# A scan's state ring widened from 8 to 16 tiles with borrowed rows, its read-outs set four slots later

## The chip, the cores and the metric

The kernel runs on one core of a Trainium2 chip. The core has five engines, each with its own instruction stream that is worked in order: TensorE (PE, matmuls; its weight loads are listed apart as PEld), VectorE (DVE), ScalarE (ACT), GpSimd (POOL) and SyncE (SP), which here only issues DMA transfers. They meet through semaphores. The metric is the time of one execution on the device in microseconds (us); a profiled execution gives the time of every instruction beside it.

## The reference

Input x is 32 sequences of 256 tokens of 256 features. A gated state-space block (a scan over time) is computed first, then two layers of windowed attention with a feed-forward part; the result is added to x. Only the scan matters here:

```python
def step(h, inputs):
    ad, bd, xt, ct = inputs
    h = jnp.clip(h * ad[:, :, None] + bd[:, :, None] * xt[:, None, :], -10.0, 10.0)
    yt = jnp.einsum('bd,bdh->bh', ct, h)
    return (h, yt)
_, ys = jax.lax.scan(step, h0, (Ad..., Bd..., xn..., Cm...))
y = ys.transpose(1, 0, 2) + D * xn
return y * jax.nn.silu(gate) @ W_out.T
```

The state h is 16 x 512 for each sequence. The 256 steps of a sequence depend on one another; the read-out yt of a step needs only that step's state.

## The kernel before

**Groups.** The 32 sequences are worked in four groups of eight (`GB = 8`). The 16 states of 8 sequences fill the 128 partitions, so one step of one group is one VectorE instruction on a 128x512 tile (`step`, line 719; line 722 in the profile). The first group's scan runs by itself ("alone": `g == 0`), before any attention can start; the scans of the other groups run beside the attention and feed-forward of the group before. The kernel has a second branch (`exact`) that these inputs don't take.

**Slots.** A scan is laid out in slots, one per step. `group_scan` fills an agenda: `at(s, what, ...)` puts a piece of work into slot s, and `scan_slots` calls the pieces slot by slot. A scheduler then places each instruction in its engine's order; it may move an instruction from where it was called, except where `tc.keep_in_program_order` holds it. 32 steps make a chunk (`CH = 32`, eight chunks c = 0 to 7, s0 = 32 c); 16 steps make a half chunk (hb).

**A step.** SP loads a row of the normalised input from DRAM, spread over 128 partitions (`load_rows`, line 691, tile xrep, six buffers); two of every eight rows are spread by TensorE instead (`spread_rows`, line 699, tile bx, from a transfer xq, line 751). ScalarE scales it (`scale_row`, line 712). VectorE adds the state and clips (line 722): a new state tile h from pool `hp`, eight buffers. The step t of a new state can start only when the tile it takes has been read out. The clip limits (`lim`, lines 666 and 667) are made on POOL once per chunk.

**Read-out.** Four steps make a block i. `read_out` (line 729, matmul in line 734) issues four matmuls, one for each state of the block, each 32 columns of weights wide, so that each lands in its own 32 rows of the bank y. In the profile an fp32 matmul is two records, so a block is eight. The call stood in slot s + 4 i + 5, where s is the first slot of the half chunk: one slot after the block's last step. The weights `ly` are written by POOL (`put_c`, line 675), one tile for each half.

**What follows a read-out.** POOL multiplies the input by D (`skip`, line 764, reads xq, writes xd, which has one buffer), VectorE adds y (`gated`, line 785), TensorE turns the tile (`out_turn`, line 791, tile tz), VectorE multiplies by the gate sg (`out_gate`, line 805, tile zT), TensorE projects (`project_y`, line 814), ScalarE copies (`copy_y`, line 825) and issues the transfer to ys in DRAM (`put_y`, line 836). The gate sg is written by ScalarE (`gate_th`, through `reorder`, line 373) into one buffer per chunk.

**Beside it on TensorE in the first scan.** The input projections of the chunk (`project`, line 401) and those of the other three groups, done ahead (`ahead_project`, line 428, tile ps_a, loaded on SP by line 417); the raw projections (line 520), the turns for the normalisation (line 550) and sums (line 624) of the next chunk. The convolution of the next chunk is on POOL (line 480) and VectorE (lines 474 and 491), its statistics on VectorE (line 560) and POOL (line 567), its normalisation on ScalarE and POOL (lines 581, 588, 589). The tiles xq and xa share four buffers of tag "rot".

**Residual rows.** Attention keeps one tile `res0` to `res7` per sequence of the group (`load_res`, line 960), 2 x 257 columns of 128 partitions, in pool `rpool`, loaded from ys after slot 256 + 18 (`DRAIN`). During the first scan they hold nothing.

Of the kernel before, what the change touches and what calls it, by code (L numbers as in the profile page):

```python
# [10 lines left out]
FP = mybir.dt.float32  # L11
# [8 lines left out]
P = 128  # L20
S = 256
DM = 256
KM = DM // P
DI = 512
# [4 lines left out]
NCH = S // CH  # L29
# [44 lines left out]
def kernel(  # L74
# [29 lines left out]
    nc = tc.nc  # L104
# [119 lines left out]
    def program(ctx, exact):  # L224
        rpool = ctx.enter_context(tc.tile_pool(name="res", bufs=1, reuse_waits="tile"))
# [3 lines left out]
        hp = ctx.enter_context(tc.tile_pool(name="hp", bufs=8, reuse_waits="tile"))  # L229
# [6 lines left out]
        def bank(pool, tag, name):  # L236
            return pool.tile([P, DI], FP, tag=tag, name=name)
# [141 lines left out]
        def group_scan(g):  # L379
# [8 lines left out]
            alone = g == 0  # L388

            agendas = [{}]  # L390
            state = {"p": one}
            ck = [{} for _ in range(NCH)]

            def at(s, what, *args):
                agendas[-1].setdefault(s, []).append(partial(what, *args))

# [288 lines left out]
            def by_tensor(t):  # L685
                return alone and t % (2 * NQ) < XR
# [31 lines left out]

            def step(c, t):
                bx = ck[c].pop(("rep", t))  # L720
                h_new = hp.tile([P, DI], FP, tag="h", name="h")
                nc.vector._custom_dve(  # L722
                    TENSOR_ADD_SAT, out=h_new, in0=state["h"], in1=bx,
                    s0=ck[c]["lim"][:, 0, t : t + 1], s1=ck[c]["lim"][:, 1, t : t + 1],
                )
                ck[c]["h", t] = state["h"] = h_new


            def read_out(c, hb, i):
                if i == 0:  # L730
                    ck[c]["y", hb] = bank(ps_w, "w", "y")
                for q in range(NQ):
                    t = i * NQ + q
                    nc.tensor.matmul(  # L734
                        ck[c]["y", hb][32 * q : 32 * q + 32, :],
                        ly[hb % 2][:, 32 * t : 32 * t + 32],
                        ck[c].pop(("h", hb * TB + t)),
                        start=(i == 0),
                        stop=(i == NI - 1),
                    )  # L740

            def load_skip(c, hb):
                if alone:
                    xd = ap_.tile([P, HEADS, DH], FP, tag="rot", name="xq", bufs=4)
                    ck[c]["xq", hb] = xd
                    xd = xd.rearrange("p h d -> p (h d)")
                else:
                    xd = ck[c]["xd"] = sp.tile([P, DI], FP, tag="xd", name="xd")
                for q in range(NQ):
                    t0 = hb * TB + q  # L750
                    nc.sync.dma_start(
                        out=xd[q * 32 : (q + 1) * 32],
                        in_=rows(c)[:, t0 : t0 + TB - NQ + 1 : NQ, :].rearrange(
                            "b i d -> i b d"
                        ),
                    )
# [96 lines left out]

            rep_w = []
            at(-1, start)
            if alone:
                at(-30, spread_weights)
                constants(at)
            for c in range(NCH):
                for t in range(CH):  # L860
                    at(c * CH + t, step, c, t)
            for c in range(NCH):
                s0 = c * CH
                for hb in range(CH // TB):
                    s = s0 + hb * TB
                    for i in range(NI):
                        at(s + 4 * i + 5, read_out, c, hb, i)
                    at(s + 21, gated, c, hb)
                    at(s + 25, out_gate, c, hb)
                    at(s + 11, skip, c, hb)  # L870
                for ch in range(NC_):
                    at(s0 - 38 + 2 * ch, conv_in, c, ch)
                    at(s0 - 37 + 2 * ch, conv_taps, c, ch)
                    at(s0 - 36 + 2 * ch, conv_th, c, ch)
                    if not alone:
                        at(s0 - 35 + 2 * ch, conv_out, c, ch)
                for ch, s in enumerate((13, 16, 17, 18)):
                    at(s0 + s + 2, gate_th, c, ch)
                    if not alone:
                        at(s0 + s + 4, gate_out, c, ch)  # L880
                at(s0 - 25, raw_copy, c)
                at(s0 - 24, raw_turn, c)
                for j in range(NJ):
                    s = s0 - 26 + 4 * j
                    at(s + 2, norm_stats, c, j)
                    at(s + 5, norm_shift, c, j)
                    at(s + 5, norm_apply, c, j)
                    at(s + 6, norm_affine, c, j)
                    at(s + 9, norm_out, c, j)
                    at(s + (9 if alone else 10), norm_put, c, j)  # L890
                at(s0 - 11, length, c)
                at(s0 - 9, figures, c)
                at(s0 - 7, figures_in, c)
                at(s0 - 6, decay_th, c)
                at(s0 - 5, decays, c)
                at(s0 - 4, put_c, c, 0)
                at(s0 + 4, put_c, c, 1)
                for d in range(KM):
                    at(s0 + 45 + 2 * d, copy_y, c, d)
                    at(s0 + 46 + 2 * d, put_y, c, d)  # L900
            agendas.append({})
            for c in range(NCH):
                s0 = c * CH
                at(s0 - 43 if alone else s0 + 6, load_x, c)
                if alone:
                    for ch in range(NC_):
                        at(s0 - 40 + 2 * ch, project, c, ch)
                else:
                    for i in range(2):
                        at(s0 - 44 + 2 * i, load_projected, c, i)  # L910
                for ch, s in enumerate((13, 16, 17, 18)):
                    at(s0 + s, project, c, NC_ + ch)
                at(s0 - 27, raw_sums, c)
                for j in range(NJ):
                    at(s0 - 26 + 4 * j, norm_turn, c, j)
                at(s0 - 8, figures_out, c)
                for t in range(CH):
                    if not by_tensor(t):
                        at(s0 + t - 6, load_rows, c, t)
                    if by_tensor(t) and t % XR == 0:  # L920
                        at(s0 + t - 4, spread_rows, c, t)
                    at(s0 + t - 2, scale_row, c, t)
                for hb in range(CH // TB):
                    s = s0 + hb * TB
                    at(s - 9 if alone else s + 7, load_skip, c, hb)
                    at(s + 23, out_turn, c)
                for d in range(KM):
                    at(s0 + 43 + 2 * d, project_y, c, d)

            if alone:  # L930
                n = (NG - 1) * NCH * 2
                for u in range(n):
                    s = -30 + u * (NCH * CH) // n
# [6 lines left out]
        def scan_slots(groups):  # L940


            slots, scans = {}, [group_scan(g) for g in groups]
            for part in range(2):
                for i, agendas in enumerate(scans):
                    for s, what in agendas[part].items():
                        slots.setdefault(i * S + s, []).extend(what)
            for s in range(min(slots), max(slots) + 1):
                for what in slots.get(s, ()):
                    what()  # L950
                yield s


        ys, res, wt, projected = {}, {}, {}, {}
# [610 lines left out]
        s0 = done[0]  # L1565
# [130 lines left out]
```

## Time and profile before

| | |
|---|---|
| runs (us) | 3534.11, 3535.7, 3530.09; median 3534.11 |
| the profiled execution | 3535.63 us, span 3533.5 us, mean granted TensorE clock 0.990 |
| first step and last of the first scan | 48.7 and some 437 us |
| chunks 0 to 7, first step to first step (us) | 51.7, 48.9, 48.8, 49.5, 48.4, 47.5, 48.3, 46.9 |
| busy in 247.6 to 296.0 us, chunk 4 (us of 48.4) | PE 46.2, PEld 25.6, DVE 42.3, ACT 32.5, POOL 17.8; DMA share 0.82 |
| chunks of the next group, beside attention (us) | 74 to 103 |

The page's busy times are sums over instructions of one engine. Matmuls are pipelined and their ends are modelled, so a busy PE is not a PE at its peak. "x8" counts records; two are one fp32 matmul here. In a view of waits a row names the engine and line that waited, after the arrow what ended the wait, then us in total, times and the longest. The chain of waits follows the work that ended last back through what released it.

### The profile page before, as it was taken

The numbers are of one execution on the slowest core, as the hardware profiler recorded it, in microseconds if no ns is written. First come the engines' busy times: TensorE is split into PE (matmuls) and PEld (weight loads), VectorE is DVE, ScalarE is ACT, GpSimd is POOL, SyncE is SP. The second block draws the span as 40 slices with busy tenths as digits, with TensorE's granted clock in tenths as the row PEclk, the third lists the DMA queues.
The fourth block names the chain that finished last, engine by engine and source line by source line (L and its number), as shares of the span: only waits on it lengthen the run. The fifth ranks groups of instructions, "written<-read, shape, count | busy, mean of one in ns | idle before, by whom it ended". The sixth has DMA issues, their size and how long they took to land.

```text
span 3533.5 us, 56484 instructions
## 1 busy us (share of the span) xinstructions
PE 3418.2 (97%) x19580; PEld 2257.4 (64%) x19580; DVE 2683.2 (76%) x5177; ACT 2035.4 (58%) x3663; POOL 1625.6 (46%) x1587
## 2 busy tenths in 40 slices
PE   7999989999999999999999999999999999999999
PEld 4545335666666666666666666666666777777777
DVE  5888898878788788888888888888787655555563
ACT  4666656656666665666666656666566444444442
POOL 4433456544455555544455555544444434333441
PEclk9999999999999999999999999999999999999999
DMA  7787655545454555444454555544444212011111
GB/s 208 215 217 218 198 169 153 136 113 142 129 143 130 150 147 151 136 114 134 117 142 128 148 148 147 137 120 130 118 142 118 61 37 62 13 31 36 37 28 38
DMA packets 487195, 436.65 MB, mean 124 GB/s; under 512 B 247155, under 2 KB 326516, under 8 KB 486772
## 3 DMA queue, kind: packets, MB, share of 16 engines
q1 hardware_dynamic: 401426, 420.41, 42.2%
q10 hardware_dynamic: 85474, 12.53, 2.1%
q8 instruction: 157, 2.57, 0.3%
q14 instruction: 138, 1.13, 0.1%
HBM read 384.06 MB, written 47.19 MB: 122 GB/s over the span
## 4 chain that ended last, share of the span: by engine, by line
PE 63%; DVE 17%; DMA 7%; POOL 5%; ACT 4%; issue 3%; SPq 1%; ACTq 0%; DVEq 0%; POOLq 0%
PE ps_qkv L996 13%; PE pa L1405 13%; DVE h L722 7%; PE po_f L1432 6%; PE y L734 5%; PE ps_wo L1052 4%; PE ov L1289 3%; DMA xrep<-xnd 3%; PE ps_out L814 3%; PE ps_in L401 3%; PE sc L1232 3%; PE tr_qk L1041 2%; PE rs L1269 2%; PE ps_raw L520 2%; DVE acc L491 1%
## 5 line engine op out<-in xcount | busy, mean ns | idle before, releaser
L722 DVE CUSTOM_DVE_ANT_0 h<-h,xrep,lim 128x512 f32<-128x512 f32 x1024 | 917.2, 896 | 137.3 <-ACT xrep L712 93.4
L712 ACT ACTIVATE xrep<-xrep,beta 128x512 f32<-128x512 f32 x960 | 671.6, 719 | 265.5 <-DMA xrep<-xnd 178.2
L996 PE MATMUL ps_qkv<-qkv,res 128*128 128x512 f32 x1536 | 716.0, 601 | 26.6 <-DVE ag L1423 12.5
L1405 PE MATMUL pa<-hT,w 128*128 128x256 f32 (+1 forms) x2816 | 674.7, 382 | 5.1 <-DVE zT L805 5.1
L1405 PEld LDWEIGHTS pa<-hT,w 128*128 128x128 f32 (+1 forms) x2816 | 517.4, 188 | 145.4 <-issue 41.8
L1020 POOL TENSOR_TENSOR rot<-rot,swp 128x512 f32<-128x512 f32 x256 | 345.1, 1348 | 496.7 <-DVE swp L1017 465.9
L996 PEld LDWEIGHTS ps_qkv<-qkv,res 128*128 128x128 f32 x1536 | 282.0, 191 | 311.5 <-issue 247.0
L1026 POOL TENSOR_TENSOR rn<-ss,neg_half 128x8 f32<-128x8 f32 x256 | 457.6, 1788 | 0.0
L734 PE MATMUL y<-h,ly 128*32 128x512 f32 x2048 | 341.1, 606 | 15.7 <-DVE h L722 13.6
L1432 PE MATMUL po_f<-ag,w 128*128 128x256 f32 x1280 | 306.7, 387 | 3.8 <-DVE fo L1443 3.1
L1423 DVE SCALAR_TENSOR_TENSOR ag<-pa,b_sb,ag 128x256 f32<-128x256 f32 x320 | 151.5, 474 | 208.7 <-ACT ag L1416 208.7
L1009 ACT ACTIVATE sq<-ps_qkv,tiny 128x512 f32<-128x512 f32 x256 | 173.3, 685 | 186.3 <-PE ps_qkv L996 129.3
L1432 PEld LDWEIGHTS po_f<-ag,w 128*128 128x128 f32 x1280 | 235.3, 190 | 68.3 <-DVE pT L1260 12.9
L1416 ACT ACTIVATE ag<-pa,b_sb 128x256 f32<-128x256 f32 x320 | 150.0, 469 | 209.7 <-PE pa L1405 206.8
L1357 POOL TENSOR_TENSOR rstd<-ve,neg_half 128x2 f32<-128x2 f32 x64 | 46.5, 726 | 484.9 <-DVE ve L1355 484.8
L1052 PE MATMUL ps_wo<-oT,wo 128*128 128x256 f32 x1024 | 231.6, 379 | 0.0
L1012 DVE TENSOR_TENSOR rot<-ps_qkv,rc_sb 128x512 f32<-128x512 f32 x256 | 175.1, 684 | 71.8 <-ACT sq L1009 70.1
L491 DVE SCALAR_TENSOR_TENSOR acc<-xr,wc_sb,acc 128x256 f32<-128x256 f32 x384 | 183.1, 499 | 50.8 <-POOL acc L480 50.0
L1017 DVE TENSOR_TENSOR swp<-ps_qkv,rs_sb 128x256 f32<-128x256 f32 x512 | 191.8, 416 | 27.6 <-POOL rot L1020 27.5
L1052 PEld LDWEIGHTS ps_wo<-oT,wo 128*128 128x128 f32 x1024 | 194.5, 190 | 27.2 <-ACT th_g L774 0.8
L1032 DVE SCALAR_TENSOR_TENSOR rot<-rn,rot 128x512 f32<-128x512 f32 x256 | 205.7, 841 | 7.5 <-POOL rn L1026 7.5
L1244 ACT ACTIVATE pT<-sc 128x512 f32<-128x512 f32 x384 | 201.6, 601 | 8.2 <-PE sc L1232 6.1
(161 smaller groups left out, 5375.6 us busy)
## 6 DMA issues: line engine op xcount, KB each, us to landing
xrep<-xnd SPq DMA_DIRECT2D x960, 256.0 KB
rb<-inv SPq DMA_DIRECT2D x128, 256.0 KB
xnd<-xn SPq DMA_DIRECT2D x64, 256.0 KB
qkv<-in_wqkv_dram SPq DMA_DIRECT2D x24, 512.0 KB
ahead<-xs_a SPq DMA_DIRECT2D x48, 256.0 KB
xp<-ahead SPq DMA_DIRECT2D x48, 256.0 KB
xd<-xnd SPq DMA_DIRECT2D x192, 64.0 KB
w<-in_w_dram SPq DMA_DIRECT2D x80, 128.0 KB
```

The lines of the kernel that those rows point to most:

```text
L491: nc.vector.scalar_tensor_tensor(acc, xr[:, :, k : k + CH], wc_sb[:, ch, k : k + 1], acc, ALU.mult, ALU.add,)
L712: scaled = nc.scalar.activation(bx, ck[c].pop(("bx", t), bx), AF.Copy, scale=ck[c]["beta"][:, t : t + 1])
L722: nc.vector._custom_dve(TENSOR_ADD_SAT, out=h_new, in0=state["h"], in1=bx, s0=ck[c]["lim"][:, 0, t : t + 1], s1=ck[c]["lim"][:, 1, t : t + 1],
L734: nc.tensor.matmul(ck[c]["y", hb][32 * q : 32 * q + 32, :], ly[hb % 2][:, 32 * t : 32 * t + 32], ck[c].pop(("h", hb * TB + t)), start=(i = ...
L996: nc.tensor.matmul(ps, res[b][:, k, t0 : t0 + W], wt["qkv", a][:, k], start=(k == 0), stop=(k == KM - 1),)
L1020: nc.gpsimd.tensor_add(rot, rot, swp)
L1026: nc.gpsimd.tensor_tensor(rn, ss, neg_half, ALU.pow)
L1032: nc.vector.scalar_tensor_tensor(rot, bc(rn, 2, DH), 1e12, rot, ALU.min, ALU.mult)
L1052: nc.tensor.matmul(po[:, d], wt["wo", 0][:, c, d * P : (d + 1) * P], oT[:, c, :], start=(c == 0), stop=(c == NC_ - 1),)
L1244: nc.scalar.activation(p, banks[r], AF.Exp)
L1405: nc.tensor.matmul(dst[x], wt["w1", m][:, k, x], self.h[:, k], start=(k == 0), stop=(k == KM - 1),)
L1432: nc.tensor.matmul(self.po[:, d], wt["w2", 0][:, m, d * P : (d + 1) * P], self.ag[m], start=(m == 0), stop=(m == len(MCH) - 1),)
```

## The change

- The first scan's state tiles: a counter n goes round 16. Even n take a tile of `hp` as before (eight buffers); odd n take the first 512 columns of `res{n // 2}`. The ring has 16 tiles.
- `later(c)` is 4 in the first scan for all chunks but the last, and 0 elsewhere. Read-outs, the addition of y, the turn, the gate's product, the projection, the copy and the store stand that many slots later.
- `skip` and the second half's `put_c` stand `later(0)` later in all chunks of the first scan, the last among them.
- The first matmul of each read-out block is held in TensorE's program order where `later(c)` is not 0.

```diff
+            def later(c):
+
+                return 4 if alone and not exact and c < NCH - 1 else 0
+
...
             def step(c, t):
                 bx = ck[c].pop(("rep", t))
-                h_new = hp.tile([P, DI], FP, tag="h", name="h")
+                n = state["n"] = (state.get("n", -1) + 1) % 16
+                if alone and not exact and n % 2:
+                    h_new = rpool.tile(
+                        [P, KM * (1 + S)], FP, tag=f"res{n // 2}", name="h_res"
+                    )[:, 0:DI]
+                else:
+                    h_new = hp.tile([P, DI], FP, tag="h", name="h")
...
-                    nc.tensor.matmul(
+                    read = nc.tensor.matmul(
...
+                    if q == 0 and later(c):
+                        tc.keep_in_program_order(read)
...
-                        at(s + 4 * i + 5, read_out, c, hb, i)
-                    at(s + 21, gated, c, hb)
-                    at(s + 25, out_gate, c, hb)
-                    at(s + 11, skip, c, hb)
+                        at(s + 4 * i + 5 + later(c), read_out, c, hb, i)
+                    at(s + 21 + later(c), gated, c, hb)
+                    at(s + 25 + later(c), out_gate, c, hb)
+                    at(s + 11 + later(0), skip, c, hb)
...
-                at(s0 + 4, put_c, c, 1)
+                at(s0 + 4 + later(0), put_c, c, 1)
                 for d in range(KM):
-                    at(s0 + 45 + 2 * d, copy_y, c, d)
-                    at(s0 + 46 + 2 * d, put_y, c, d)
+                    at(s0 + 45 + 2 * d + later(c), copy_y, c, d)
+                    at(s0 + 46 + 2 * d + later(c), put_y, c, d)
...
-                    at(s + 23, out_turn, c)
+                    at(s + 23 + later(c), out_turn, c)
                 for d in range(KM):
-                    at(s0 + 43 + 2 * d, project_y, c, d)
+                    at(s0 + 43 + 2 * d + later(c), project_y, c, d)
```

## The prediction

> **What bounds the kernel now.** I read the page first: its engine shares, its slices and the costliest groups.
>
> ```profile
> span 3533.5 us, 56484 instructions
> PE 3418.2 (97%) x19580; PEld 2257.4 (64%) x19580; DVE 2683.2 (76%) x5177; ACT 2035.4 (58%) x3663; POOL 1625.6 (46%) x1587
> L722 DVE CUSTOM_DVE_ANT_0 h<-h,xrep,lim 128x512 f32<-128x512 f32 x1024 | 917.2, 896 | 137.3 <-ACT xrep L712 93.4
> L734 PE MATMUL y<-h,ly 128*32 128x512 f32 x2048 | 341.1, 606 | 15.7 <-DVE h L722 13.6
> ```
>
> TensorE is full from end to end, so an average says little; what counts is the stretch that the diff touches. The records of line 722 put the 256 steps of the first scan between 48.7 and 438.7 us: eight chunks of 46.9 to 51.7 us, about 1.5 us a step. The instruction order of the changed program differs from the old one only there; after it the same instructions follow in the same order on every engine, and TensorE is full again from about 500 us. So a microsecond won or lost in the first scan should come out at the end as one microsecond, and I work on these 390 us alone.
>
> Next, the view of windows, for the first and second part of two chunks (columns: stretch, its length, then busy us of PE, weight loads, DVE, ACT, POOL, clock, DMA share, GB/s).
>
> ```profile
> 202.50:223.70 21.20, 21.20 (x93) 11.00 (x93) 17.88 (x26) 14.24 (x27) 9.21 (x8) 1.00 0.89 233
> 223.70:247.60 23.90, 21.05 (x85) 11.93 (x85) 19.32 (x40) 14.00 (x27) 7.05 (x13) 0.86 0.82 214
> 251.60:272.90 21.30, 21.30 (x101) 11.19 (x102) 19.04 (x29) 16.06 (x31) 8.29 (x8) 1.00 0.89 228
> ```
>
> In the first part of a chunk (21 us) TensorE has no gap and VectorE idles 3.3 and 2.3 us; in the second part TensorE has gaps. The chain of waits through the same place says why:
>
> ```profile
> 202.50 1.04 PE y L734 x2
> 203.55 1.01 PE ps_raw L520 x4
> 204.56 0.97 PE y L734 x2
> ...
> 209.29 1.28 PE y L734 x6
> ...
> 211.16 0.97 PE y L734 x2
> ...
> 217.04 0.99 PE y L734 x8
> ...
> 221.69 2.01 PE y L734 x8
> ```
>
> A read-out is four matmuls (eight records) on four separate column groups. Together they take 0.99 us; one alone (x2) takes 0.97 to 1.04. Where a state is not yet written, the four are issued in two or three pieces with other work between, and each piece costs as much as the whole. The chain stays on TensorE from 202.5 to 223.7, then goes to a step, a row load of 4.8 us, ScalarE, steps, another load: the second part is paced by those. Last the view of waits over the whole scan (us, times, longest):
>
> ```profile
> PEld y L734 <- DVE h L722: 34.9, 45, 2.3
> POOL xd L764 <- PE tz L791: 26.3, 12, 4.3
> ```
>
> ```profile
> DVE h L722 <- ACT xrep L712: 12.9, 16, 3.4
> DVE acc L491 <- POOL acc L480: 11.7, 23, 1.7
> ...
> DVE st L560 <- PE tp_x L550: 6.1, 5, 1.4
> ...
> DVE xr L474 <- PE ps_in L401: 2.1, 3, 1.3
> ...
> DVE h L722 <- PE y L734: 1.4, 4, 0.7
> ```
>
> TensorE waits for states; VectorE waits little for TensorE.
>
> **The change, part by part.** No arithmetic, matmul or DMA is added: 256 steps, 256 read-out matmuls, the same loads. Edits of place only.
>
> *Read-outs four slots later, the first of each four held in TensorE's order.* In the changed order every block of chunks 0 to 6 stands in one piece: 56 pieces for 56 blocks, where it was 70 (10, 8, 10, 10, 10, 10, 12). Chunk 7, which is not moved, goes from 13 pieces to 20. What the pieces cost on the chain in the five first parts of chunks 2 to 6: chunk 3 spends 7.26 us on four blocks (1.04+0.97+1.28+0.97+0.99+2.01), against 4 x 1.0: 3.3 us. Read the same way, chunk 2 has 5.7 for three, 2.7; chunk 4 has 6.2 for four, 2.2; chunk 5 has 6.3, 2.3; chunk 6 has 6.2, 2.2. Sum -12.7 us. Chunks 0 and 1 show no such pieces on the chain: 0. The check against VectorE: it idles 2.3 to 3.3 us in these parts, so it can just follow; it is what is late next, and it forbids more than this there.
>
> *Ring of 16.* Step n waits for the read-out of step n-16 instead of n-8. That takes away the 1.4 us of steps waiting for y and a 0.5 us one of line 785: -2. Writing every second state into a residual row is the same instruction on the same shape: 0. The next loads of these rows come after the last read-out and after ys is written, so they wait for ys as now: 0; if a residual load were held up, each step late there would cost one 1.5 us.
>
> *TensorE's other waits for h.* Of the 34.9 us, 17.4 fall before 391 us (the same view over 48.7 to 391); the rest fall in chunk 7 and past it, where TensorE has time to spare. Of the 17.4, the five first parts hold 1.1, 2.3, 0.5, 0.5 and 1.2, so 5.6, already within their pieces. Bounds for the 11.8 left: 0, and -12. I take -4, nearer to nothing, because in the second part of chunk 3 the chain is on TensorE for 9.2 of 23.9 us.
>
> *Chunk 7.* Seven more pieces, each up to 0.75 us of TensorE (1.0 less a quarter of a block): at most +5; TensorE idles 5.7 us in the chunk, so I take +1.
>
> *Skip, gating, turns, projections four slots later.* The products of line 764 (1.27 us on POOL, two per chunk) move. The first stays between a turn and the statistics of the next chunk: 0, bounds -0.5 and +0.5 a chunk. The second goes from a quiet place (230 us) to one between the first convolution product of line 480 and the clip limits (lines 666, 667), where POOL was waiting 2.35 us for VectorE; 1.27 fits, so it is hidden if tz is there in time. Behind it stand the limits, ly and the next convolution product, for which VectorE waits. Two inputs on POOL slow a step beside them: 1.69 us beside line 764 at 207.8 us against 0.80 alone. So bounds 0 and +0.9 a chunk, I take +0.4, seven times: +3. The transfers xq wait for this product too; the row loads behind them on SP's queue are six slots ahead, so 0 here, and the rival below prices it. ScalarE's writes of sg now follow their last reader by two slots instead of six: 0, as ScalarE runs about two slots ahead, bound +2 over the scan. put_c of the second half moves with its reader: 0.
>
> Sum: -12.7 - 2 - 4 + 1 + 3 = -14.7 us. The profiled execution took 3535.6 (span 3533.5 and 2.1 around it), so 3520.9 for its like; it stands 1.5 above the median of the runs, 3534.1, so 3519.4: **3519 us**.
>
> [...]
>
> **Rivals.**
>
> *Hidden.* VectorE, the row loads (DMA busy 0.89) and POOL pace the scan, and TensorE's time turns into waiting. For it: VectorE busy 42 of 48 us per chunk and 11.7 us of its waits are for POOL. Against: the chain runs 21 us on TensorE in five chunks. Then only the -2 of the ring and the +4 of the losses remain: 3536, with its like between 3527 and 3541.
>
> *Slower, by the moved skip on POOL.* Place: the second product of line 764, which waits for tz on TensorE, with the limits, ly, the next convolution product and the next xq transfer behind it. POOL's wait for tz has a mean of 2.2 us (26.3 by 12) and a longest of 4.3. If it is waited where POOL has no slack, a chunk loses 2.2 + 1.27 = 3.5 us, seven times 24.5, against -17.7 without the +3: 3534 + 7 = 3541; with the longest, (4.3 + 1.27) x 7 = 39: 3555. It decides from 17.7 / 7 = 2.5 us a chunk on. Against it: in the built order tz stands ahead of the bx matmuls that wait for xq.
>
> *More.* All 34.9 us and the 2 come back, because the whole scan goes at TensorE's pace: 3497. For it: the chain lies on TensorE or on what waits for it in most of 198 to 400 us. Against: VectorE's 6 us of idle a chunk include 11.7 us for POOL and 6.9 for ad over the scan.
>
> *Not doing what it says* (pieces still split, because only the first of each four is held): the built order shows whole blocks, so I give it no share of its own; it would look like Hidden.
>
> **How the numbers follow.** This kernel's runs spread over 0.16%, so 0.2% (7 us) is about what can be told from no change: 3527 to 3541 is "same". Forecast 0.50 (own range 3507 to 3527), More 0.12, Hidden 0.16, Slower 0.22. Faster 0.62, same 0.16, slower 0.22. The range 3498 to 3543 leaves out some 0.05 below (most of More lies just under or over 3498) and 0.15 above.
>
> **What would show it.** In the changed profile: read-outs of 0.99 to 1.08 us in records of x8 from 48 to 390 us and no lone pairs; TensorE's wait for h in chunks 0 to 6 near 0; steps not waiting for y; chunks 2 to 6 at 45.5 to 46.5 us instead of 47.5 to 49.5; chunk 7 within 2 us of 46.9; everything later shifted by the same amount. Wrong, if chunks keep their length while waits for xrep or for POOL grow (Hidden), or if POOL's wait for tz sits ahead of the limits (Slower).

## The result, and the profile after

| | kernel before | changed kernel |
|---|---|---|
| median of ten runs each (us) | 3533.18 (3530.09 to 3545.35) | 3543.73 (3537.56 to 3557.71) |
| ratio, 95% interval | | 1.0033 (1.0016 to 1.0049) |
| the profiled execution: run, span (us) | 3535.6, 3533.5 | 3537.6, 3535.7 |
| first scan: its first step, first step of the next group (us) | 48.7, 438.7 | 48.4, 443.5 |
| chunks 0 to 7 (us) | 51.7 48.9 48.8 49.5 48.4 47.5 48.3 46.9 | 56.1 49.6 46.4 49.4 47.1 47.6 50.3 48.7 |
| from the last step of the last scan to the end (us) | 783.7 | 783.6 |

The change makes the kernel slower, by some 10 us at the median. The profiled execution shown here is the fastest of its ten; a second one, of `after_again` below, took 3546.2 us, with a scan of 400.0 us (50.4 to 450.4) in which TensorE idled for 51.6 us.

The page of the changed kernel: its span, busy times, and the groups of the steps and of the read-outs. In the first scan every step now writes or reads `h_res`; those steps, and the read-outs of `h_res`, are groups of their own, so the counts below are smaller than before.

```profile
span 3535.7 us, 56480 instructions
PE 3405.2 (96%) x19580; PEld 2254.7 (64%) x19580; DVE 2673.7 (76%) x5177; ACT 2035.9 (58%) x3663; POOL 1634.3 (46%) x1587
L732 DVE CUSTOM_DVE_ANT_0 h<-h,xrep,lim 128x512 f32<-128x512 f32 x769 | 678.4, 882 | 113.3 <-ACT xrep L716 83.3
L744 PE MATMUL y<-h,ly 128*32 128x512 f32 x1792 | 311.5, 611 | 9.7 <-DVE h L732 9.6
```

TensorE is busy for 13.0 us less than before (3418.2), and yet the span is longer. The view of windows for the whole first scan shows where. First the kernel before, then the changed one, whose second and third rows are the two parts of chunk 3 from read-out to read-out (columns as in the prediction's windows).

```profile
48.70:438.70 390.00, 363.56 (x1545) 187.06 (x1544) 335.08 (x592) 251.08 (x459) 155.37 (x202) 0.96 0.77 211
```

```profile
48.40:443.50 395.10, 349.55 (x1545) 183.04 (x1544) 330.94 (x592) 250.57 (x459) 159.08 (x209) 0.94 0.77 208
206.90:228.90 22.00, 21.91 (x105) 12.90 (x105) 19.23 (x29) 17.41 (x34) 9.09 (x9) 0.92 0.85 235
228.90:253.40 24.50, 19.64 (x90) 10.51 (x91) 18.92 (x42) 12.55 (x23) 8.90 (x17) 0.93 0.81 207
```

TensorE's busy time in the scan fell from 363.6 to 349.6 us: 14.0 us less, close to the 12.7 us that the forecast had for the pieces. Its idle time grew from 390.0 - 363.6 = 26.4 to 395.1 - 349.6 = 45.5 us: 19.1 us more. The difference, 5.1 us, is what the scan lost.

The chain of waits through chunk 3 of the changed kernel shows both halves of this (start us, us, what):

```profile
198.83 1.19 POOL acc L484
200.04 0.28 DVE acc L495
200.32 4.79 DMA xrep<-xnd
...
205.20 0.60 ACT xrep L716
...
205.85 0.72 ACT xrep L716
206.57 0.32 ACT xc L505
...
206.93 0.65 PE ps_raw L524 x2
...
210.23 1.53 PE y L744 x8
...
215.76 1.00 PE y L744 x8
...
220.41 1.00 PE y L744 x8
...
227.84 1.03 PE y L744 x8
228.89 0.82 DVE h_res L732
...
232.12 2.64 SPq L448
...
234.85 4.87 DMA xrep<-xnd
239.75 0.68 ACT xrep L716
```

Every read-out of chunks 0 to 6 is one piece now, here 1.00 to 1.03 us (1.53 for the one that ran partly at half clock, see below), so four blocks cost 4.6 us where they cost 7.3. But the chain isn't on TensorE any more at the start of the chunk, 200 to 207 us: it is on a row load, then on ScalarE, and TensorE waits. Later, at 232 us, SP's queue stands for 2.64 us at the issue of one store (line 448), and the row load behind it is issued only at 234.85. The timeline around the first of these places (start, us, engine, line, operation; in brackets the idle time before and what ended it):

```profile
205.20 1.37 ACT L716 ACTIVATE xrep<-xrep,beta 128x512 f32<-128x512 f32 x2 [2.33 <-DMA xrep<-xnd]
205.84 0.47 DVE L495 SCALAR_TENSOR_TENSOR acc<-xr,wc_sb,acc 128x256 f32<-128x256 f32 x1
...
206.47 0.40 ACT L505 ACTIVATE xc<-acc 128x256 f32<-128x256 f32 x1
...
206.93 0.65 PE L524 MATMUL ps_raw<-xc,wx_sb 128*64 128x256 f32 x2 [2.44 <-ACT xc L505]
```

ScalarE has idled 2.33 us for the row, then scales two rows and makes xc, for which TensorE has idled 2.44 us. The rows hardly held xc here: what it reads, the last of VectorE's convolution taps (line 495), ended only at 206.31 (205.84 + 0.47), 0.16 us before xc began. In all six waits of TensorE for xc in this scan (9.9 us) xc began within 0.3 us of its last tap, but for one with 0.6 us; in `after_again` it began 1.0 to 1.8 us after its tap, behind scaled rows, in four of eight. In the kernel before the split read-outs stood at this place (the lone pairs at 202.50 and 204.56 in the prediction's chain). The same view of the kernel before, for the same xc and the matmuls that read it:

```profile
204.39 0.40 ACT L501 ACTIVATE xc<-acc 128x256 f32<-128x256 f32 x1
...
205.46 1.08 PE L520 MATMUL ps_raw<-xc,wx_sb 128*64 128x256 f32 x4
```

The four records are the last two of the four matmuls of ps_raw. The one that reads the last xc began at 205.95, 1.16 us after xc was done; in chunks 2 to 6 this margin was 0.95 to 1.53 us. A piece taken away ahead of it could give back that much and no more before TensorE waited for xc, if xc comes when it did.

The views of waits for the scan, VectorE first, then TensorE (us, times, longest):

```profile
DVE ad L658 <- ACT ad L653: 13.0, 5, 3.4
DVE h L732 <- ACT xrep L716: 9.9, 7, 7.0
DVE h_res L732 <- ACT xrep L716: 9.8, 13, 1.6
DVE acc L495 <- POOL acc L484: 8.6, 20, 1.1
...
DVE st L564 <- PE tp_x L554: 2.1, 3, 0.8
...
PE ps_st L628 <- DVE rhs L619: 10.2, 4, 6.2
PE ps_raw L524 <- ACT xc L505: 9.9, 6, 2.5
PE ps_in L405 <- DMA xg<-in_xT_dram: 8.0, 5, 2.5
PE ps_a L432 <- DMA xa<-in_xT_dram: 7.9, 6, 2.2
```

VectorE waits 4.0 us less for turned tiles (6.1 to 2.1). It waits 6.8 us more for scaled rows (12.9 to 9.9 + 9.8) and 6.1 us more for ad (6.9 to 13.0), which ScalarE makes behind scaled rows. ScalarE's own wait for rows to land grew from 81.6 to 99.1 us.

### The profile page after: what moved, and what is told of

Read it like the earlier page. It is cut to its first block, busy times and chain, and to the rows that moved or that the text cites. A ratio compares the mean times of both kernels' runs of the same rounds, so it can differ in the third digit from the quotient of the medians.

```text
span 3535.7 us, 56480 instructions
## 1 busy us (share of the span) xinstructions
PE 3405.2 (96%) x19580; PEld 2254.7 (64%) x19580; DVE 2673.7 (76%) x5177; ACT 2035.9 (58%) x3663; POOL 1634.3 (46%) x1587
## 4 chain that ended last, share of the span: by engine, by line
PE 61%; DVE 18%; DMA 8%; POOL 5%; ACT 4%; issue 3%; SPq 1%; ACTq 0%; DVEq 0%; POOLq 0%
PE ps_qkv L1008 13%; PE pa L1417 13%; PE po_f L1444 6%; DVE h L732 6%; PE ps_wo L1064 4%; PE y L744 4%; PE ov L1301 3%; DMA xrep<-xnd 3%; PE ps_out L826 3%; PE ps_in L405 3%; PE sc L1244 3%; PE tr_qk L1053 2%; DVE acc L495 2%; PE rs L1281 2%; DMA xp<-ahead 2%
## 5 line engine op out<-in xcount | busy, mean ns | idle before, releaser
L732 DVE CUSTOM_DVE_ANT_0 h<-h,xrep,lim 128x512 f32<-128x512 f32 x769 | 678.4, 882 | 113.3 <-ACT xrep L716 83.3
L744 PE MATMUL y<-h,ly 128*32 128x512 f32 x1792 | 311.5, 611 | 9.7 <-DVE h L732 9.6
L1444 PEld LDWEIGHTS po_f<-ag,w 128*128 128x128 f32 x1280 | 236.1, 191 | 68.7 <-DVE pT L1272 12.9
L1029 DVE TENSOR_TENSOR swp<-ps_qkv,rs_sb 128x256 f32<-128x256 f32 x512 | 191.8, 416 | 28.4 <-POOL rot L1032 28.3
L484 POOL TENSOR_SCALAR acc<-xr,wc_sb,bconv_sb 128x256 f32<-128x256 f32 x128 | 102.8, 806 | 228.8 <-DVE xr L478 108.7
```

The lines of the kernel that those rows point to most:

```text
L732: nc.vector._custom_dve(TENSOR_ADD_SAT, out=h_new, in0=state["h"], in1=bx, s0=ck[c]["lim"][:, 0, t : t + 1], s1=ck[c]["lim"][:, 1, t : t + 1],
L744: read = nc.tensor.matmul(ck[c]["y", hb][32 * q : 32 * q + 32, :], ly[hb % 2][:, 32 * t : 32 * t + 32], ck[c].pop(("h", hb * TB + t)), sta ...
L1029: nc.vector.tensor_mul(swp[:, :, o], ph[:, :, s], bc(rs_sb[:, l, w, a, o], 1, HEADS))
L1444: nc.tensor.matmul(self.po[:, d], wt["w2", 0][:, m, d * P : (d + 1) * P], self.ag[m], start=(m == 0), stop=(m == len(MCH) - 1),)
```

## The experiments

Each ratio is to runs of the kernel before on the same chip. Their median is 3540.39 us for the first four kernels below; 3537.87 for `after_again`, `fill_after`, `fill_elsewhere` and `fill_before`; 3540.06 for `loads_early`, `tanh_held` and the two with short rows; 3540.80 for `half_y_before`, `fill_raw` and the two with a ring for rows; 3538.04 for the two with a tap less. A ratio is taken from all runs and can differ by 0.001 from the quotient of two medians. The changed kernel's own comparison is `after_again` and the table above.

**Which part of the change.** One part alone or one part undone.

`ring_only`, the ring of 16 with no work moved or held:

```diff
-                return 4 if alone and not exact and c < NCH - 1 else 0
+                return 0
```

> The ring of 16 alone, every slot and order call as before. Theory (the read-outs' new places change the chunk's end: row loads and the tanh pace it, and TensorE idles in larger lumps at half clock): the ring alone changes little, 3533 us within 5, and 6 to 9 half-clock stretches before 390 us as before (7), not the 13 of the changed kernel. Rival (the borrowed rows themselves cost, by where they lie or by what waits for their release): 3540 us or more, chunk 0 longer by 4 us as in the changed kernel.

Measured 3542.02 us, ratio 1.0001 (0.9991 to 1.0012).

`no_hold`, the ring and the later slots without the hold:

```diff
-                    if q == 0 and later(c):
+                    if False:
```

> The changed kernel without holding the first matmul of a block in TensorE's order. Theory (later read-outs): if the scheduler pulls the blocks forward again, the order is near the old one and the time 3530 to 3536 us. Rival (the four slots alone, held or not, cause the loss): 3540 us or more.

Measured 3544.03 us, ratio 1.0015 (1.0002 to 1.0027).

`hold_only`, the kernel before and only the hold:

```diff
-                    nc.tensor.matmul(
+                    read = nc.tensor.matmul(
...
+                    if q == 0 and alone and not exact and c < NCH - 1:
+                        tc.keep_in_program_order(read)
```

> The kernel before with only the hold on the first matmul of a block in chunks 0 to 6: ring of 8, old slots. Theory: TensorE now waits for each block's states with other work behind it, 3545 to 3560 us, more waits of TensorE for h than 34.9 us. Rival (pieces of read-outs were the cost, as the prediction had it): whole blocks, 3520 to 3530 us.

Measured 3543.63 us, ratio 1.0006 (0.9995 to 1.0017).

`put_later`, the changed kernel with the store of line 448 four slots later:

```diff
-                    at(s + 4, ahead_put, u)
+                    at(s + 8, ahead_put, u)
```

> The changed kernel with the stores of the projections done ahead issued four slots later on SP's queue, so that the row loads do not stand behind their wait for ScalarE. Theory (row loads behind SP's waits pace the chunk's end): 5 to 12 us off the changed kernel, 3532 to 3539 us. Rival (the clock or TensorE's order alone): no change, 3543 us within 4.

Measured 3549.74 us, ratio 1.0020 (1.0008 to 1.0032). The idea that the store of line 448 in SP's queue is the whole cause fell: moved, it brought nothing.

`after_again`, the changed kernel on the chip of the next three:

> The changed kernel once more, on the chip of the three runs beside it, so that they can be compared with it and not only with the kernel before. Both theories: 3538 to 3552 us, a ratio of 1.000 to 1.004 to the kernel before; in its profile 10 to 14 half-clock stretches of 3.4 or 6.8 us in the first scan.

Measured 3546.78 us, ratio 1.0022 (1.0009 to 1.0035). The ring alone costs nothing; with the read-outs later the loss is there, with the hold or without it.

**Is it TensorE's clock?** The granted clock in the scan fell from 0.96 to 0.94. In the clock records of the two profiled executions of the table TensorE's granted clock is 0.50 in stretches of 3.4 or 6.8 us: 34 us in six stretches before, 51 us in twelve after. One such stretch, the third row, follows the 2.44 us wait just shown (windows of the changed kernel):

```profile
199.00:202.40 3.40, 3.40 (x20) 1.26 (x19) 3.10 (x8) 1.56 (x4) 1.47 (x4) 1.00 0.54 189
...
205.80:207.90 2.10, 0.97 (x5) 0.56 (x6) 2.10 (x5) 1.11 (x4) 0.66 (x1) 0.99 1.02 238
207.90:211.30 3.40, 3.40 (x14) 1.54 (x12) 3.34 (x8) 2.24 (x4) 0.53 (x1) 0.50 1.08 261
```

And the time of single runs goes with the clock: of the changed kernel's ten, four have a mean granted clock of 0.984 and take 3551.5 to 3557.7 us, six have 0.987 to 0.990 and take 3537.6 to 3544.8. So the next runs fill TensorE's waits with matmuls that nobody reads.

`fill_after`, and `fill_raw` with the first of the two hunks alone:

```diff
+                    if ch == NC_ - 1 and alone and not exact:
+                        fill = bank(ps_w, "w", "fill")
+                        for _ in range(4):
+                            nc.tensor.matmul(
+                                fill[:, 0:256], ident, ck[c]["xc"][:, ch - 1],
+                                start=True, stop=True,
+                            )
...
+                pst = bank(ps_w, "w", "ps_st")
+                if alone and not exact:
+                    for _ in range(4):
+                        tc.keep_in_program_order(
+                            nc.tensor.matmul(
+                                pst[:, 256:512], ident, w_in_sb[:, 0, 0:256],
+                                start=True, stop=True,
+                            )
+                        )
```

> The changed kernel with eight more matmuls in each chunk of the first scan, whose results nobody reads: four between the third and the last ps_raw (the 2.4 us gap of slot 4) and four ahead of ps_st. They cost TensorE about 3.4 us a chunk, 27 us in all. Clock theory (TensorE's waits now come in lumps, and its granted clock halves after a lump): the lumps of slot 4 go, the half-clock stretches of the scan fall from 12 to 6 or fewer, and the time falls to 3525-3538 us, although TensorE does more. Rival (the loss is in TensorE's order and the chain, the clock only goes along with it): the added matmuls are paid where they aren't hidden, 3550-3575 us, half-clock stretches as before.

> The changed kernel with only the first four of fill_after's added matmuls, whose results nobody reads, in slot 4 before the last ps_raw, where TensorE waits 2.4 us. Clock theory (the lump costs by the half clock that follows it): no half-clock stretch begins in slots 4-6, and the time is 3-10 us below the changed kernel's 3544-3547 us. Rival (any TensorE work added in this scan is paid, the clock stretch comes elsewhere): 5-20 us slower than the changed kernel, as many stretches.

`fill_elsewhere`, four such matmuls ahead of each group of ps_out in `project_y`:

> The control: the changed kernel with the same number of added matmuls, read by nobody, but ahead of the groups of ps_out in project_y (chunks 0 to 6), where TensorE is busy anyway. Clock theory: the lumps and the half-clock stretches (10 to 14) stay, the added matmuls cost up to 3.4 us a chunk, 3550-3570 us, in any case not faster than the changed kernel by more than 3 us. Rival that any more TensorE work raises the mean clock and so the speed: faster by as much as the run with the matmuls in the gaps.

`fill_before`, the kernel before with four ahead of the first bx of a chunk:

> The kernel before with four added matmuls, read by nobody, ahead of the first bx of each chunk after the first, where its profile has a gap of 1.2-1.8 us and its half-clock stretches begin. Clock theory: six half-clock stretches of the scan become two or fewer, 34 us at half clock become 10 or fewer, and the time falls by 3-12 us (ratio 0.997-0.999). Rival (the clock only goes along): the same to 1.7 us x 7 = 12 us slower.

| | median us | ratio (95%) | first scan us | PE busy in it | half-clock stretches in it |
|---|---|---|---|---|---|
| fill_after | 3583.24 | 1.0122 (1.0107 to 1.0138) | 429.7 | 381.8 | 13, 61 us |
| fill_raw | 3561.48 | 1.0067 (1.0053 to 1.0080) | 410.0 | 355.9 | 9, 58 us |
| fill_elsewhere | 3577.28 | 1.0118 (1.0097 to 1.0138) | 435.3 | 375.6 | 15, 79 us |
| fill_before | 3545.99 | 1.0020 (1.0011 to 1.0029) | 400.3 | 371.1 | 5, 20 us |

The clock theory's times fell in all four. The stretches that began in slots 4 to 6 did go in `fill_after` and `fill_raw`, but others came in slots 22 to 30, behind waits that hadn't been there, and the added matmuls were paid in full or more (32 us busy, 35 us of scan in `fill_after`), in the gaps as well as elsewhere. In `fill_before` the half-clock time did fall, from 34 to 20 us, and the kernel got slower by the added work. These runs don't separate the clock from the work they add.

**Is it the loads' lead, or the tanh behind the rows?**

`loads_early`:

```diff
-                at(s0 - 43 if alone else s0 + 6, load_x, c)
+                at(s0 - 45 if alone else s0 + 6, load_x, c)
...
-                    at(s - 5, ahead_load, u)
+                    at(s - 8, ahead_load, u)
```

> The changed kernel with xa loaded eight slots ahead of ps_a instead of five and xg 45 slots ahead instead of 43; nothing else. Theory (loads end last): TensorE's waits for xa and xg (15.9 us) fall to 6 us or less and 3-10 us come back, 3532-3541 us. Rival (these waits only stand in for others): the waits move to ps_raw and ps_st, the time stays within 3 us of the changed kernel's 3544-3547.

Measured 3546.25 us, ratio 1.0021 (1.0010 to 1.0033). TensorE's waits for xa are gone and those for xg are next to nothing (0.9 us), and its idle time is the same 45.6 us: above all the waits for xq (1.6 to 8.4 us) and for xc (9.9 to 13.6) grew. The rival's expectation came true: those waits only stood in for others.

`tanh_held`, line 653 held in ScalarE's order:

```diff
-                nc.scalar.activation(ad, ck[c]["bcd"][:, 2], AF.Tanh, bias=wbias[:, 2:3])
+                th = nc.scalar.activation(ad, ck[c]["bcd"][:, 2], AF.Tanh, bias=wbias[:, 2:3])
+                if alone and not exact:
+                    tc.keep_in_program_order(th)
```

> The changed kernel with one more instruction held in its engine's order: the tanh of the decays on ScalarE (L653), which in the changed kernel comes late behind rows at the chunk's end (VectorE waits 13.0 us for it in all, 6.9 us in the kernel before). Theory (it is a place where the gain is given back): VectorE's wait for ad falls to 7 us or less and 3-6 us come back, 3538-3543 us. Rival (the tanh waits for the same rows anyway): no change, 3544-3548 us.

Measured 3544.94 us, ratio 1.0015 (1.0003 to 1.0027); VectorE's wait for ad is 16.8 us. In its order the tanh still stands behind scaled rows: each of the five times that VectorE waits for it, it starts right after a row for which ScalarE had idled 1.2 to 4.6 us, or after a second row behind such a one. The rival fits; a tanh ahead of those rows wasn't tried.

**What does a microsecond of each resource bring?** These runs need no moved read-out: they take time off one resource of the kernel before (and two of them off the changed kernel too). Each leaves out work that the result needs, so only its time is of use.

`half_y_before` (TensorE), read-outs over half the columns, the half added twice:

```diff
-                        ck[c]["y", hb][32 * q : 32 * q + 32, :],
+                        ck[c]["y", hb][32 * q : 32 * q + 32, 0 : DI // 2 if alone and not exact else DI],
...
```

> The kernel before with its read-outs over 256 of the 512 columns (L734), and the half added twice, so that VectorE's work stays and the other half of y is left out. It takes 15-25 us of TensorE's time out of the first scan and moves nothing to another slot. The step of the forecast that a us off TensorE is a us off the scan: 15-25 us faster than the kernel before, 3515-3525 us. Theory (TensorE doesn't set the scan's pace alone; what it saves turns into waits for rows, copies and loads): within 6 us of the kernel before, TensorE's idle time in the scan 12 us or more above 26 us.

Measured 3544.36 us, ratio 1.0012 (0.9999 to 1.0025). Its scan in the view of windows, and from its views of waits VectorE's wait for scaled rows:

```profile
50.40:444.10 393.70, 350.29 (x1545) 191.50 (x1544) 322.84 (x593) 248.19 (x459) 155.65 (x202) 0.94 0.79 209
```

```profile
DVE h L722 <- ACT xrep L712: 33.1, 29, 7.0
```

This is the changed kernel's picture without the change: TensorE busy 350.3 (13.3 us less than before), idle 43.4, clock 0.94, half-clock time 48 us in ten stretches, and no gain. VectorE is busy for 12.2 us less as well (its steps take 888 ns in the mean instead of 928), and its wait for scaled rows went from 12.9 to 33.1 us: neither engine's saved time came back.

`taps_before` and `taps_after` (VectorE), one of three convolution taps left out:

```diff
-                for k in range(1, TAPS):
+                for k in range(2 if alone and not exact else 1, TAPS):
```

> The kernel before with one of the three convolution taps on VectorE left out in the first scan (L491: 32 instructions of 495 ns, 16 us of VectorE's time). Theory (VectorE, busy 335 of the scan's 390 us, sets the pace together with the rows): 8-16 us faster than the kernel before, 3524-3533 us. Rival (the rows' bytes and waits for them alone): within 4 us of it.

> The same tap left out of the changed kernel (L495). Theory (VectorE sets the pace in both kernels): 8-16 us faster than the changed kernel's 3544-3547 us, and still not below taps_before. Rival (in the changed kernel TensorE's waits have another origin): within 4 us of the changed kernel. If TensorE's saving shows as soon as VectorE has less to do: below taps_before by 5 us or more.

Measured 3540.25 us, ratio 1.0005 (0.9990 to 1.0020), and 3552.74 us, ratio 1.0041 (1.0026 to 1.0056). VectorE is busy for 14.3 us less in the scan of `taps_before` (320.8), for 12.5 less in that of `taps_after`, and neither is faster: VectorE's time alone doesn't set the pace either. In `taps_before` its wait for scaled rows went from 12.9 to 28.4 us.

`rows_short_before` and `rows_short_after` (the rows' bytes), 16 of a row's 512 columns loaded and a constant tile scaled in the row's place:

```diff
-                nc.sync.dma_start(out=xr, in_=bc(rows(c)[:, t, :], 0, NS))
+                n = 16 if alone and not exact else DI; nc.sync.dma_start(out=xr[:, 0:n], in_=bc(rows(c)[:, t, 0:n], 0, NS))
...
-                    bx, ck[c].pop(("bx", t), bx), AF.Copy, scale=ck[c]["beta"][:, t : t + 1]
+                    bx, ck[c].pop(("bx", t), dskip_sb if alone and not exact else bx), AF.Copy, scale=ck[c]["beta"][:, t : t + 1]
```

> The kernel before with only 16 of the 512 columns of each broadcast row loaded (L691), and ScalarE scaling dskip_sb in the row's place, so that the rows of the scan are wrong and a row is there early. It is the base line of rows_short_after. Theory (row loads): ScalarE's waits for rows (81.6 us in the first scan) fall below 20 us; the scan gets shorter by 5-20 us, 3515-3535 us. Rival (TensorE alone sets the old kernel's pace): within 5 us of the kernel before.

> The same edit on the changed kernel (L695): 16 columns of each row loaded, dskip_sb scaled instead, the scan's rows wrong. Theory (TensorE's 20 us were saved, but the row loads and the other loads and copies behind them on SP's queue end last now, so the saving turned into waits): without the rows' bytes the saving shows, 10-20 us below rows_short_before. Rival (clock: TensorE waits in lumps of its own making and its clock halves): still no gain on rows_short_before, within 5 us of it or slower, with 10 or more half-clock stretches in the scan.

Measured 3519.19 us, ratio 0.9941 (0.9924 to 0.9958), and 3525.46 us, ratio 0.9958 (0.9944 to 0.9973). The scans, first of the one and then of the other, and TensorE's largest wait in the second:

```profile
50.20:424.30 374.10, 356.73 (x1545) 178.39 (x1544) 338.46 (x594) 246.04 (x459) 159.41 (x202) 0.99 0.38 90
```

```profile
60.30:434.50 374.20, 335.93 (x1543) 178.46 (x1544) 336.12 (x591) 246.72 (x459) 157.26 (x209) 0.95 0.38 90
```

```profile
PE ps_raw L524 <- ACT xc L505: 22.8, 13, 3.2
```

Without the rows' bytes (DMA share 0.38 instead of 0.77) each kernel gets about 20 us faster: the only resource of the three whose time comes back. But the read-outs' saving still doesn't show. TensorE is busy for 20.8 us less in the second scan, and both last 374 us: now it waits 22.8 us for xc, and ScalarE waits 17.7 us for VectorE's acc to make it. That the row loads alone hide the saving is thus refuted; behind them stands the convolution's path over POOL, VectorE and ScalarE. TensorE was also at half clock for 38 us in the second scan against 10 in the first, so a share of the clock isn't ruled out here. (Left out, the bytes also shift the scheduler's order at some places in both kernels.)

**The same memory for the rows.** `xring_only` gives the residual rows' memory in the kernel before to the scan's rows, a ring of 14 tiles; `xring_8` also issues the loads in slot t - 8 instead of t - 6:

```diff
+            def row_tile():
+                n = state["n"] = (state.get("n", -1) + 1) % 14
+                if alone and not exact and n % 7 > 2:
+                    return rpool.tile(
+                        [P, KM * (1 + S)], FP, tag=f"res{n // 7 * 4 + n % 7 - 3}", name="x_res"
+                    )[:, 0:DI]
+                return xp.tile([P, DI], FP, tag="xrep", name="xrep")
...
-                xr = xp.tile([P, DI], FP, tag="xrep", name="xrep")
+                xr = row_tile()
...
-                    ck[c]["rep", t] = xp.tile([P, DI], FP, tag="xrep", name="xrep")
+                    ck[c]["rep", t] = row_tile()
```

> The kernel before with the residual rows' memory given to the rows of the scan instead of to its states: a ring of 14 tiles for xrep instead of 6, loads in the same slots. If SP's queue is held up by xrep's buffers (its waits for the step that frees one are 53 us in the scan): 0-6 us faster than the kernel before. If the loads' own transfer sets their landing (DMA share 0.77): no change.

> The ring of 14 for xrep, and the row loads issued eight slots ahead of their step instead of six. Theory (the rows' late landing is worth up to the 20 us that the kernel before gains without their bytes): ScalarE's wait for rows (81.6 us) falls to 50 us or less, VectorE's for scaled rows (12.9 us) to 6 us or less, 5-15 us faster than the kernel before, 3522-3533 us. Rival (the bytes themselves, not the lead, cost the 20 us): within 4 us of the kernel before.

`xring_only`: 3531.97 us (3529.09 to 3543.00), ratio 0.9982 (0.9972 to 0.9992), faster than the kernel before, and so than the changed one. `xring_8`: 3538.01 us, ratio 0.9997 (0.9987 to 1.0008); with the same ring and the longer lead the gain is gone, and why is open. From `xring_only`, the window of the scan and ScalarE's waits for rows:

```profile
50.00:438.50 388.50, 364.71 (x1544) 180.37 (x1544) 339.19 (x593) 247.25 (x459) 159.45 (x210) 0.99 0.80 213
```

```profile
ACT xrep L720 <- DMA xrep<-xnd: 34.8, 23, 4.1
ACT x_res L720 <- DMA x_res<-xnd: 23.3, 21, 3.0
```

ScalarE waits 58.1 us for rows instead of 81.6, TensorE's waits over 1 us are 4 with 7.4 us instead of 11 with 15.3, and its clock in the scan is 0.99. TensorE is busy as long as before. Of the uses of that memory measured here this is the one that paid, by 0.2% and with the loads in their old slots only.

## Why the prediction was wrong

**A microsecond of the scan is a microsecond at the end: right, to some 3 us.** The first scan ends 4.8 us later in the changed profile and the last scan 2.2 us later; in that of `after_again` 11.7 and 10.9. What follows the last step takes as long as before (783.6 and 783.7 us).

**Pieces of read-outs, -12.7 us: the step that failed.** The pieces went, as forecast, and TensorE's busy time fell by 14.0 us. What failed is "what the pieces cost on the chain" taken as time that comes back. Chunks 2 to 6 got shorter by 1.7 us together (242.5 to 240.8), not by 12.7; in the profile of `after_again` they are 4.9 us longer (247.4). The chain of the kernel before lay on TensorE for 21 us of a chunk, but xc, at the end of a second path over POOL's and VectorE's convolution and ScalarE, which also has rows to scale, was ready only 0.95 to 1.53 us ahead of it. The forecast took 2.2 to 3.3 us off each of these chunks; with the pieces gone xc ends last. The prediction's check for what is late next looked at VectorE's 2.3 to 3.3 us of idle time and not at what xc and the rows wait for. `half_y_before` shows it without the change: 13.3 us off TensorE, none off the kernel. And less time in read-outs doesn't mean less time of the kernel: in the first scan TensorE is busy with them for 111.1 us in the kernel before, for 96.2 in the changed one and for 130.5 in `xring_only`, the fastest of the three.

**TensorE's other waits for h, -4: the waits went, the time didn't.** Weight loads waited 17.4 us for states in chunks 0 to 6, now 3.0 + 3.2; the time turned up in other waits (ps_raw, ps_st, ps_a, ps_in: 39.6 us in the chunks before the last, against 9.0 in the whole scan of the kernel before).

**Ring, -2: not there.** `ring_only` is at 1.0001. The steps' waits for y went from 1.4 to 0.2 us, but xd (line 797) waits 3.1 us for y instead of 0.5.

**Chunks 0 and 1, 0: wrong.** They lost 4.4 and 0.7 us. Chunk 0 is about as long where no slot is moved (57.0 in `half_y_before`, 54.9 in `taps_before`), so the moved slots need not be its cause.

**Chunk 7, +1: right.** 46.9 to 48.7, +1.8, inside its bounds.

**The moved skip on POOL, +3, and the rival that it makes the kernel slower: wrong.** POOL's wait for tz fell from 26.3 to 17.3 us (26.1 in `after_again`), its limits' wait for ct from 20.0 to 10.2 (12.8), VectorE's for acc from 11.7 to 8.6 (7.1): the limits behind the moved product still wait for ct, and VectorE waits no longer than before for what POOL makes behind it. The result lies in that rival's range, but not by its mechanism.

**Sum.** 3519 us was forecast and 3543.7 measured: -14.7 was forecast for the scan, +5.1 and +10.0 were measured in the two profiled executions of the changed kernel (395.1 and 400.0 against 390.0). Hidden, with a chance of 0.16, named what happened as far as the hidden time goes: chunks 2 to 6 nearly keep their length while waits for xrep grow. Its 3536 us is 8 us too low, since it counted only what is hidden and no loss. The loss beyond it goes with TensorE's half-clock stretches in the changed kernel (51 us against 34 in the kernel before); `half_y_before` has them too (48 us), with a ratio (0.9999 to 1.0025) that doesn't tell a loss from none. Whether they cause the loss or only follow the waits the runs don't settle: its cause stays open.

## What to carry to other kernels

Time on the chain of waits is an upper bound for what a change can bring: before counting on it, ask of the instruction behind the removed one what it waits for and when that ends, here xc, done about 1 us ahead of TensorE behind convolution taps and scaled rows. The cheapest test of a supposed bound is to take a like amount of time off it without moving anything, and to do the same to the other candidates; of TensorE, VectorE and the rows' bytes only the last answered. Of two uses of the same free memory, buffers for the transfers whose landing was waited for brought 0.2%, and buffers that allowed later read-outs cost 0.2 to 0.3%.

## What the hardware showed

In the first scan of the table's two profiled executions TensorE's granted clock went to 0.50 for 3.4 or 6.8 us at a time. In the changed kernel's scan eleven such stretches begin after the first step. The 3.4 us ahead of nine of them hold 0 to 41% of matmul time; for eight of the nine the longest wait was 1.7 to 2.5 us, and the ninth began within a wait of 6.2 us. The other two had 64 and 73%. The wait of 2.44 us shown above was followed by 3.4 us at 0.50. Two kernels with the same matmuls and nearly the same idle time of TensorE in the scan, 26.4 us in the kernel before and 23.8 in `xring_only`, had 34 and 7 us of half clock, so the sum of the waits alone doesn't tell it; the longer waits differ, 15.3 and 7.4 us in waits over 1 us.
